# First block of layer 1 in a two-layer attention kernel: bank order, engine orders, three projections kept in their banks, first expert layer in halves

## The chip, the cores and the metric

The kernel runs on one core of one Trainium2 chip. The core has TensorE (PE: matmuls and transposes; its weight loads are listed as PEld), VectorE (DVE), ScalarE (ACT), GpSimd (POOL), and SyncE (SP), which issues the DMAs of this kernel. Each engine takes its instructions in program order and waits on semaphores for those of other engines. TensorE writes to PSUM, which is used here as eight banks of 128 partitions x 512 f32 each.

The metric is the time of one execution in device microseconds. The kernel before took 1599.19 us, the median of three runs (1595.45 to 1604.54).

## The reference, cut to what matters

The input x has 32 x 128 tokens (n, t) of 256 channels, f32. Layer 0 is attention over all 4096 tokens with a mask on t, then an output projection. Layer 1 normalises, adds a windowed attention, normalises again, and adds a mixture of eight experts that all work on every token.

```python
# layer 0, h = x[(1, 32, 128, 256)]
x0 = layernorm(h); q = x0 @ wq.T + bq + sym_emb[n]
Q, K, V = heads(q @ wQ.T + bQ), heads(h @ wK.T + bK), heads(h @ wV.T + bV)   # 8 heads of 32
scores = einsum('bqhd,bkhd->bhqk', Q, K) / sqrt(32)
scores = where(t_key > t_query, -inf, scores)
ctx = einsum('bhqk,bkhd->bqhd', softmax(scores), V)
t = h + alpha * (ctx @ out_w.T + out_b)
...
# layer 1, on t[(1, 4096, 256)]
x = layernorm(t)
logits = relu((x @ K) @ x.T + bias)
window = (i - 12 <= j) & (j < i + 12)
t = t + softmax((logits - 10000 * (1 - window)) * temperature) @ x
x = layernorm(t)
w = softmax(x @ Wr + br)                        # eight weights a token
for e in range(8):
    h1 = relu(bn1(x @ W1[e] + b1[e]))
    h2 = relu(bn2(h1 @ W2[e] + b2[e]))
    t = t + w[:, e] * (h2 @ Wo[e] + bo[e])
```

## The kernel before

**Tiles and blocks.** The 4096 tokens are 32 tiles of 128 (tile n holds the t = 0..127 of one n) and eight blocks of four tiles (`TPB` = 4, 512 tokens). Block b is tiles 4b to 4b+3. `groups[b]` is the same shifted by one, tiles 4b+1 to 4b+4 (tiles 0 to 4 for b = 0), because the window of a tile reaches 16 tokens (`SIDE`) into the next one.

**Layer 0** runs first, over blocks, groups of four heads and key tiles; it fills most of the first 750 us. At its end `close_sums` makes the last softmax sums in one bank; DVE takes their reciprocals in three parts (L1327) and multiplies them into the last columns of `big_t` (L1328), which then holds the attention output, transposed.

**Layer 1, its first block.** It is written out by hand, a list of calls in the order in which every engine gets its instructions (L1915 to 1985). The steps of a tile or a pair of tiles, with their lines:

- `project` (L1533): two matmuls of 256 columns, one for each half of the 256 channels (`project_half`), the output projection of layer 0; DVE adds the residual (L1543), `tile_stats` takes mean and variance (L1528, L1529).
- `deviations` in two parts: part 0 adds eps on DVE (L1515) and takes the square root on ACT (L1518); part 1 is the reciprocal and mean times it, negated, on DVE (L1520, L1521). One call covers several tiles. The Sqrt and the Exp of ACT are in different tables, so a load of 1.28 us stands where they alternate.
- `normalise` (L1560): ACT writes xl, the normalised tile. Then two DMAs on SP copy its first and last 16 rows (L1564, L1566) into the tiles xh of the neighbours, one for two tiles.
- `turn` (L1571, L1572): two transposes on PE, a copy to `big_t` on ACT.
- `key` (L1580, L1585): half of the keys of a block, two matmuls of 512 columns, copy on ACT.
- `logits` (L1592; DVE L1607, 1612, 1613): 160 scores for each token of a tile, threshold and mask, minus the maximum. `exponentials` (L1619) on ACT.
- `turn_weights` (L1628 to 1634): for a pair of tiles, three transposes of the softmax weights, then a copy on ACT (L1633) and one on DVE (L1634) to ptl.
- `apply` (L1641, L1645, L1651): weights times xl, then weights times the side rows xh, for two tiles; DVE divides, adds the residual and takes the next statistics.
- `expert_tokens` (L1683, xf on DVE), `turn_tokens` (L1692, four transposes; L1696, the copy to half of xfT on ACT): the input of the experts for two tiles.
- `route` (L1704, L1709): 8 small matmuls for the router's logits.

**Layer 1, the loop.** For each block and each of eight experts: `layer` W2 of this expert (L1760, four matmuls of 512 columns; relu on ACT, L1765), a call of `insert()`, `layer` W1 of the next expert, `insert()`, `combine` (L1779, L1787), `insert()`. So there are 24 points a block. `insert()` places jobs of the blocks to come, the same steps as above: it goes through the list in order, takes at most four a point, each at least one point after the jobs that it needs, and takes one that has a cost only while the cost spent is below an even share:

```python
    POINTS = 3 * E * (NBLK - 1) - 8
    total = sum(j[1] for j in jobs)
    ...
            if cost and spent >= total * (point + 1) / POINTS:
                k += 1
                continue
```

In the first block, tiles 0 to 15 are projected, and tiles 0 to 6 normalised and turned, before the loop starts; the rest are jobs.

**Banks.** `bank()` gives the PSUM bank of each of these steps from three pools, "h" with three banks, "y" with two and "x" with three, in the order of `spare["tags"]`; in the loop it gives "x" only. A bank that is given again waits until its last readers are done.

**Queues.** SP issues, in this order: K of the layer-1 attention (Ksb), tokens of block 4, Wr (L1488, after POOL has cleared its tile, which POOL does after 16 calls of `with_bias`, L904), br, bo, the expert weights (L1477, 24 loads of 256 KB) with three token loads between them (L896), and then the xh copies as `normalise` calls them. POOL adds the output bias to tokens (`with_bias`) and makes the shifts of the batch norms (L1667 to 1670).

## Time and profile before

| what | value |
|---|---|
| median of three runs | 1599.19 us (1595.45 to 1604.54) |
| the profiled execution | 1596.23 us |
| its span, first to last instruction | 1594.2 us |
| mean granted TensorE clock | 0.990 |
| busy time PE | 1532.1 us, 96% of the span |
| busy time DVE, ACT, POOL | 885.3, 878.7, 106.7 us |
| chain of work that ended last, PE's share | 88% |
| layer 0 until the last sums are closed (first 747 us) and layer 1 after it (847 us) | 1594 us |

The page also cuts the span into slices (40 slices of 39.9 us, busy share in tenths, then the granted clock in tenths, DMA's busy share and GB/s):

```profile
PE   7899899999999999998789999999999999999998
PEld 5333232232222222222446556565565656556555
DVE  4676779888898898998623223233232432223211
ACT  3666777878878878986343433334333333333322
POOL 1110003000000000003400000000000000000000
PEclk9999999999999999999889999999999999999999
DMA  4210000000000010000600000000000000000000
```

PE is at eight or nine tenths nearly everywhere. The slices that matter here are the nineteenth to the twenty-first: there DVE falls from nine tenths to two or three, as layer 0 ends, PE falls to seven or eight, its clock to eight, and the DMA engines have their one busy slice after the start, with the expert weights.

The granted clock is the share of its full rate at which TensorE was allowed to run. A matmul record of 256 columns comes every 0.2165 us at full clock and every 0.4265 us at half; an f32 matmul of this kernel leaves two records, a transpose one.

### The profile page before, as it was taken

Reading aid. Unit: us, or ns where it says so; the run is one execution under the profiler, and the core shown is the slowest. Engines: PE = TensorE matmul, PEld = TensorE weight load, DVE = VectorE, ACT = ScalarE, POOL = GpSimd, SP = SyncE. Lnnn points to the kernel's source line nnn. Section 1 sums busy time; section 2 is a strip of 40 time slices with the busy share of each in tenths; the row PEclk is TensorE's granted clock in tenths of the full one; section 3 lists DMA queues with packets and bytes.
Section 4 is the critical chain, followed back from the end, with each engine's and each line's share of the span. In section 5 each row is a group of like instructions: output and inputs, shape, how many; then the busy total and the mean of one; then the engine's idle time right before and its main releaser. Section 6 shows DMA issues by size and latency. Waiting matters only on the chain.

```text
span 1594.2 us, 20898 instructions
## 1 busy us (share of the span) xinstructions
PE 1532.1 (96%) x8163; PEld 707.6 (44%) x8163; DVE 885.3 (56%) x1508; ACT 878.7 (55%) x1162; POOL 106.7 (7%) x295
## 2 busy tenths in 40 slices
PE   7899899999999999998789999999999999999998
PEld 5333232232222222222446556565565656556555
DVE  4676779888898898998623223233232432223211
ACT  3666777878878878986343433334333333333322
POOL 1110003000000000003400000000000000000000
PEclk9999999999999999999889999999999999999999
DMA  4210000000000010000600000000000000000000
GB/s 107 61 28 18 21 8 24 8 21 8 2 8 8 1 47 21 1 8 21 203 4 4 14 1 4 14 0 17 0 0 17 1 9 8 1 15 0 14 0 15
DMA packets 36343, 30.51 MB, mean 19 GB/s; under 512 B 10007, under 2 KB 34318, under 8 KB 36238
## 3 DMA queue, kind: packets, MB, share of 16 engines
q1 hardware_dynamic: 35088, 28.02, 6.3%
q8 instruction: 66, 1.08, 0.3%
q10 hardware_dynamic: 1150, 1.09, 0.3%
q14 instruction: 39, 0.32, 0.1%
HBM read 23.63 MB, written 4.32 MB: 18 GB/s over the span
## 4 chain that ended last, share of the span: by engine, by line
PE 88%; ACT 4%; DVE 2%; issue 2%; DMA 1%; POOL 1%; SPq 0%; DVEq 0%; POOLq 0%; ACTq 0%
PE psh L1760 28%; PE sa L1246 16%; PE av L1290 14%; PE psy L1779 14%; PE psq L981 2%; ACT pt L1260 2%; PE psv L996 2%; PE psk L968 2%; PE psk L1580 2%; PE sb L1246 1%; ACT pt L1258 1%; PE sums L1316 1%; PE pso L1533 1%; PE pss L1592 1%; DMA tokens<-in_x_dram 1%
## 5 line engine op out<-in xcount | busy, mean ns | idle before, releaser
L1280 DVE TENSOR_TENSOR acc<-acc,pt 128x1024 f32<-128x1024 f32 (+3 forms) x500 | 525.1, 1116 | 43.8 <-ACT pt L1260 31.7
L1765 ACT ACTIVATE h<-psh,bshift,bscale 128x512 f32<-128x512 f32 x256 | 198.6, 776 | 395.1 <-PE psh L1760 395.1
L1260 ACT ACTIVATE pt<-sb 128x1536 f32<-128x1536 f32 (+3 forms) x288 | 387.6, 1346 | 3.3 <-PE sb L1246 3.2
L1246 PE MATMUL sa<-q,kT 32*128 32x512 f32 (+3 forms) x576 | 302.2, 604 | 7.3 <-ACT pt L1258 5.3
L1246 PE MATMUL sb<-q,kT 32*128 32x512 f32 (+3 forms) x1728 | 306.1, 604 | 2.2 <-ACT pt L1260 1.1
L1290 PE MATMUL av<-pt,v 128*32 128x512 f32 (+3 forms) x2304 | 286.2, 569 | 2.7 <-POOL pt L1264 1.3
L1787 DVE SCALAR_TENSOR_TENSOR tokens<-psy,w,tokens 128x256 f32<-128x256 f32 x256 | 111.9, 479 | 260.0 <-PE psy L1779 259.9
L1760 PE MATMUL psh<-xfT,W_sb 128*128 128x512 f32 x512 | 233.7, 599 | 0.7 <-ACT xfT L1696 0.7
L1779 PE MATMUL psy<-Wo_sb,h 128*128 128x256 f32 x1024 | 233.0, 380 | 0.4 <-ACT h L1765 0.4
L1760 PE MATMUL psh<-h,W_sb 128*128 128x512 f32 x512 | 231.4, 595 | 0.0
L1258 ACT ACTIVATE pt<-sa 128x512 f32<-128x512 f32 (+3 forms) x288 | 162.3, 563 | 95.1 <-PE sb L1246 70.9
L1779 PEld LDWEIGHTS psy<-Wo_sb,h 128*128 128x128 f32 x1024 | 192.1, 190 | 40.3 <-issue 16.1
L1246 PEld LDWEIGHTS sa<-q,kT 32*128 32x128 f32 x576 | 84.2, 183 | 217.5 <-ACT pt L1258 178.1
L1760 PEld LDWEIGHTS psh<-xfT,W_sb 128*128 128x128 f32 x512 | 95.6, 192 | 111.7 <-issue 109.0
L1760 PEld LDWEIGHTS psh<-h,W_sb 128*128 128x128 f32 x512 | 94.9, 190 | 99.0 <-issue 96.2
L1290 PEld LDWEIGHTS av<-pt,v 128*32 128x32 f32 x2304 | 45.4, 108 | 201.8 <-issue 182.8
L1264 POOL MEMSET pt<- 32x128 f32 (+2 forms) x192 | 58.5, 304 | 658.9 <-ACT pt L1260 574.5
L1246 PEld LDWEIGHTS sb<-q,kT 32*128 32x128 f32 x1728 | 88.0, 183 | 9.5 <-ACT pt L1260 6.9
L1280 DVE TENSOR_TENSOR acc<-pt,pt 128x1024 f32<-128x1024 f32 (+1 forms) x32 | 36.7, 1188 | 35.5 <-ACT pt L1260 30.6
L1607 DVE SCALAR_TENSOR_TENSOR s<-pss,negb,bandb 128x144 f32<-128x144 f32 x64 | 16.1, 293 | 53.7 <-PE pss L1592 53.7
L1651 DVE SCALAR_TENSOR_TENSOR tokens<-psa,sum,tokens 128x256 f32<-128x256 f32 x32 | 14.9, 466 | 53.0 <-PE psa L1645 53.0
L1533 PE MATMUL pso<-woT,big_t 128*128 128x256 f32 x128 | 38.3, 441 | 5.2 <-DVE rec_last L1327 5.2
(219 smaller groups left out, 911.8 us busy)
## 6 DMA issues: line engine op xcount, KB each, us to landing
xg<-in_x_dram SPq DMA_DIRECT2D x32, 128.0 KB
tokens<-in_x_dram SPq DMA_DIRECT2D x8, 512.0 KB
W_sb<-in_L_ffn_W_dram SPq DMA_DIRECT2D x16, 256.0 KB
out_dram<-tokens SPq DMA_DIRECT2D x32, 128.0 KB
rec<-flat SPq DMA_DIRECT2D x60, 64.0 KB
xs<-in_x_dram SPq DMA_DIRECT2D x24, 128.0 KB
Wo_sb<-in_L_ffn_Wo_dram SPq DMA_DIRECT2D x8, 256.0 KB
xh<-xl SPq DMA_DIRECT2D x62, 16.0 KB
```

The lines of the kernel that those rows point to most:

```text
L968: nc.tensor.matmul(ps, lhsT=wKT[:, c, g * P : (g + 1) * P], rhs=hT[:, c, :], start=(c == 0), stop=(c == 1),)
L1246: nc.tensor.matmul((sb[:, h - 1, :] if h else sa)[:, lo:], lhsT=kT[rows, g, j * P : (j + 1) * P], rhs=q[rows, g, lo:], start=True, stop=True,)
L1258: nc.scalar.activation(pt[:, 0, lo:], sa[:, lo:], AF.Exp, scale=SCALE)
L1260: nc.scalar.activation(pt[:, 1:, lo:], sb[:, :, lo:], AF.Exp, scale=SCALE)
L1264: nc.gpsimd.memset(pt[k * N : (k + 1) * N, :, lo : lo + k * N], 0.0)
L1280: nc.vector.tensor_tensor(live[b, g][:, hs, lo:], old[:, hs, lo:], pt[:, hs, lo:], op=ALU.add)
L1290: nc.tensor.matmul(av[h * HD : (h + 1) * HD, lo:], lhsT=v[:, j, (g * HG + h) * HD : (g * HG + h + 1) * HD], rhs=pt[:, h, lo:], start=(j == ...
L1533: nc.tensor.matmul(ps, lhsT=big_t[:, c, SIDE + n * P : SIDE + (n + 1) * P], rhs=woT[:, c, :], start=(c == 0), stop=(c == 1),)
L1760: nc.tensor.matmul(ps, lhsT=W[name][:, e, c, m * P : (m + 1) * P], rhs=src[:, c, :], start=(c == 0), stop=(c == 1),)
L1765: nc.scalar.activation(dst[:, m, :], ps, AF.Relu, bias=bshift[:, m, k : k + 1], scale=bscale[:, m, k : k + 1],)
L1779: nc.tensor.matmul(ps[:, k, :], lhsT=ht[:, c, r * P : (r + 1) * P], rhs=W["Wo"][:, e, c, :], start=(c == 0), stop=(c == 1),)
L1787: nc.vector.scalar_tensor_tensor(out=tokens(n), in0=ps[:, k, :], scalar=w[:, r, e : e + 1], in1=tokens(n), op0=ALU.mult, op1=ALU.add,)
```

## The change

It does six things:

1. The order of the bank tags becomes x, x, h, x, and then a cycle; the first four banks of the first block then lie outside the pool banks in which the last sums were made. Four tiles, not five, have their two matmuls apart; tile 4 is projected whole, after them.
2. The calls of the first block come in another order: the first two `normalise` ahead of the second `deviations`; three more together; `key` ahead of the projections of tiles 7 and 8 and of the batch norms; `logits(1)` ahead of `exponentials(0)`; the second `turn_weights` ahead of the square root of the second norm; `expert_tokens` earlier.
3. Tiles 9, 10 and 11 are projected into banks where they stay (`kept`); DVE adds and measures them after both halves of xf.
4. The first layer of the first expert is computed in two halves of 256 columns (`layer_halves`), the first of them before the second half of xfT is turned. `route(0)` comes after it as before.
5. The projections of tiles 12 to 15, and normalise and turn of tiles 5 and 6, are jobs of the loop instead.
6. `insert()` asks `allowed()`: the cost of block b's jobs is due by point 24b - 10, evenly between these marks.

```diff
@@ -1464,7 +1464,7 @@
     ps_h = ctx.enter_context(tc.tile_pool(name="ps_h", bufs=3, space=PSUM))
     ps_y = ctx.enter_context(tc.tile_pool(name="ps_y", bufs=2, space=PSUM))
     ps_x = ctx.enter_context(tc.tile_pool(name="ps_x", bufs=3, space=PSUM))
-    spare = {"tags": itertools.cycle("xhyxhyxh")}
+    spare = {"tags": itertools.chain("xxhx", itertools.cycle("yhxyhxhx"))}
 
     def bank(name):
         tag = next(spare["tags"])
@@ -1535,11 +1535,13 @@
             start=(c == 0), stop=(c == 1),
         )
 
-    def project(n, ps=None):
-        if ps is None:
-            ps = bank(f"pso{n}")[:, :D]
-            project_half(n, 0, ps)
-        project_half(n, 1, ps)
+    def project(n):
+        ps = bank(f"pso{n}")[:, :D]
+        for c in range(2):
+            project_half(n, c, ps)
+        finish(n, ps)
+
+    def finish(n, ps):
         nc.vector.tensor_tensor(tokens(n), ps, tokens(n), op=ALU.add)
         tile_stats(n, "st6b_")
 
@@ -1751,6 +1753,28 @@
         for r, ps in both:
             n = b * TPB + r
             nc.vector.tensor_tensor(tokens(n), ps, tokens(n), op=ALU.add)
+
+    def layer_halves(src, name, l, b, e, parts=2):
+
+        pss = [ps_h.tile([P, BLK], F32, tag="h", name=f"psh{l}_{b}_{e}_{m}") for m in range(2)]
+        for part in range(parts):
+            cols = slice(part * BLK // parts, (part + 1) * BLK // parts)
+            for m in range(2):
+                for c in range(2):
+                    nc.tensor.matmul(
+                        pss[m][:, cols], lhsT=W[name][:, e, c, m * P : (m + 1) * P],
+                        rhs=src[:, c, cols], start=(c == 0), stop=(c == 1),
+                    )
+            if part < parts - 1:
+                yield
+        dst = fh.tile([P, 2, BLK], F32, tag=f"h{l}", name=f"h{l}_{b}_{e}")
+        k = l * E + e
+        for m in range(2):
+            nc.scalar.activation(
+                dst[:, m, :], pss[m], AF.Relu,
+                bias=bshift[:, m, k : k + 1], scale=bscale[:, m, k : k + 1],
+            )
+        yield dst
 
     def layer(src, name, l, b, e):
         dst = fh.tile([P, 2, BLK], F32, tag=f"h{l}", name=f"h{l}_{b}_{e}")
@@ -1912,77 +1936,87 @@
     def tiles(b):
         return range(b * TPB, (b + 1) * TPB)
 
-    halves = {n: bank(f"pso{n}")[:, :D] for n in groups[0]}
-    for n in groups[0]:
+    first_free = 0
+
+    def project_next():
+        nonlocal first_free
+        project(first_free)
+        first_free += 1
+
+    def whole(n):
+
+        ps = bank(f"pso{n}")[:, :D]
+        for c in range(2):
+            project_half(n, c, ps)
+        return ps
+
+
+    halves = [bank(f"pso{n}")[:, :D] for n in range(TPB)]
+    for n in range(TPB):
         project_half(n, 0, halves[n])
-    for n in groups[0]:
-        project(n, halves.pop(n))
+    for n in range(TPB):
+        project_half(n, 1, halves[n])
+        finish(n, halves[n])
         if n == 1:
             deviations(range(0, 2), 0)
         if n == 2:
             deviations(range(0, 2), 1)
-    first_free = groups[0][-1] + 1
-
-    def project_next():
-        nonlocal first_free
-        project(first_free)
-        first_free += 1
-
-    deviations(range(2, TPB + 1), 0)
     normalise(0)
     normalise(1)
+    project(TPB)
+    first_free = TPB + 1
+    deviations(range(2, TPB + 1), 0)
     turn(0)
     turn(1)
-    project_next()
     deviations(range(2, TPB + 1), 1)
-    normalise(2)
+    for n in range(2, TPB + 1):
+        normalise(n)
     project_next()
     turn(2)
-    normalise(3)
+    project_next()
     turn(3)
-    normalise(4)
+    turn(4)
     for b in range(TPB, NBLK):
         for n in tiles(b):
             with_bias(n)
-    turn(4)
+    key(0, 0)
+    key(0, 1)
     project_next()
     project_next()
     deviations(groups[1], 0)
     batch_norms()
-    key(0, 0)
-    key(0, 1)
     deviations(groups[1], 1)
-    project_next()
-    project_next()
+
     logits(0)
+    logits(1)
     exponentials(0)
-    logits(1)
     exponentials(1)
-    project_next()
     logits(2)
     exponentials(2)
+    kept = [(first_free, whole(first_free))]
     turn_weights(0)
     logits(3)
     exponentials(3)
-    project_next()
+    kept.append((first_free + 1, whole(first_free + 1)))
     apply(0)
+    turn_weights(1)
     deviations(range(0, 2), 0)
-    turn_weights(1)
-    project_next()
+    kept.append((first_free + 2, whole(first_free + 2)))
+    apply(1)
     deviations(range(0, 2), 1)
+    deviations(range(2, TPB), 0)
     expert_tokens(0, 0)
-    project_next()
-    apply(1)
-    deviations(range(2, TPB), 0)
-    turn_tokens(0, 0)
-    for n in groups[1][:2]:
-        normalise(n)
     deviations(range(2, TPB), 1)
     expert_tokens(0, 1)
-    for n in groups[1][:2]:
-        turn(n)
-    project_next()
+    turn_tokens(0, 0)
+    for n, ps in kept:
+        finish(n, ps)
+    first_free += len(kept)
+    a = layer_halves(blk[0]["xfT"], "W1", 0, 0, 0)
+    next(a)
     turn_tokens(0, 1)
+    a = next(a)
+    route(0)
 
 
 
@@ -1993,7 +2027,7 @@
 
     for n in range(first_free):
         done_at["project", n] = -9
-    for n in range(groups[1][2]):
+    for n in groups[0]:
         done_at["normalise", n] = done_at["turn", n] = -9
     for g in (0, 1):
         done_at["dev0", g] = done_at["dev", g] = -9
@@ -2076,12 +2110,30 @@
 
 
     work = [(b, e) for b in range(NBLK) for e in range(E)]
-    a = layer(blk[0]["xfT"], "W1", 0, 0, 0)
-    route(0)
     spare["tags"] = itertools.cycle("x")
-    POINTS = 3 * E * (NBLK - 1) - 8
-    total = sum(j[1] for j in jobs)
     point, spent = 0, 0.0
+
+
+
+    dues, share = [(0, 0.0)], {b: 0.0 for b in range(1, NBLK)}
+    for name, cost, f, needs in jobs:
+        own = isinstance(name, tuple) and isinstance(name[1], int)
+        b = name[1] if own else 1
+        if own and name[0] in ("project", "normalise", "turn"):
+            b = max(1, (b - 1) // TPB)
+        elif own and name[0] in ("logits", "exp"):
+            b //= TPB
+        elif own and name[0] in ("weights", "apply"):
+            b //= TPB // 2
+        share[b] += cost
+    for b in range(1, NBLK):
+        dues.append((3 * E * b - 10, dues[-1][1] + share[b]))
+
+    def allowed():
+        for (p0, c0), (p1, c1) in zip(dues, dues[1:]):
+            if point < p1:
+                return c0 + (c1 - c0) * (point + 1 - p0) / (p1 - p0)
+        return dues[-1][1]
 
     def insert():
 
@@ -2089,7 +2141,7 @@
         k = few = 0
         while k < len(jobs) and few < 4:
             name, cost, f, needs = jobs[k]
-            if cost and spent >= total * (point + 1) / POINTS:
+            if cost and spent >= allowed():
                 k += 1
                 continue
             if all(done_at.get(q, point) < point for q in needs if q in known):
```

## The prediction

> **What bounds the kernel now.** I read the windows by engine first, to see which stretch can be shortened at all; the columns are the stretch, its length, busy time and count of PE, PE weight load, DVE, ACT and POOL, then granted clock, DMA share and GB/s.
>
> ```profile
> core 0: us, PE busy (x) PEld busy (x) DVE busy (x) ACT busy (x) POOL busy (x), PEclk, DMA share, GB/s
> 747.60:764.50 16.90, 7.62 (x24) 5.83 (x20) 11.24 (x25) 0.27 (x2) 13.30 (x22) 0.80 0.23 73
> 764.50:787.60 23.10, 18.36 (x69) 13.19 (x69) 12.00 (x42) 8.88 (x21) 13.56 (x22) 0.85 0.96 309
> 787.60:812.20 24.60, 17.06 (x68) 9.65 (x67) 11.54 (x42) 7.16 (x17) 0.00 (x0) 0.72 0.02 4
> 812.20:1594.20 782.00, 774.53 (x2774) 463.65 (x2767) 228.17 (x715) 285.30 (x450) 6.63 (x36) 1.00 0.02 7
> ...
> ```
>
> From 812.2 to the end PE is busy 774.53 of 782.00 us at full clock: the loop over experts costs what its matmuls cost, and work moved into it pays its whole PE time. Only the 64.6 us before it have slack, PE being busy 43.0 of them, part of that at a clock of 0.72 to 0.85.
>
> Second, PE's timeline in that stretch (start, duration, line, tiles, count; in brackets the idle time and who ended it):
>
> ```profile
> 752.84 7.55 PE L1533 MATMUL pso<-woT,big_t 128*128 128x256 f32 x20 [5.18 <-DVE rec_last L1327]
> 765.23 1.18 PE L1571 MATMUL ptx<-ident,xl 128*128 128x128 f32 x4 [4.84 <-ACT xl L1560]
> ...
> 776.49 3.60 PE L1580 MATMUL psk<-big_t,Ksb 128*128 128x512 f32 x8
> ...
> 788.16 1.13 PE L1641 MATMUL psa<-xl,ptl 128*128 128x256 f32 x4 [0.36 <-ACT ptl L1633]
> 789.22 0.70 PE L1645 MATMUL psa<-xh,ptl 32*128 32x256 f32 x4
> ...
> 794.60 1.13 PE L1641 MATMUL psa<-xl,ptl 128*128 128x256 f32 x4 [2.34 <-ACT ptl L1633]
> ...
> 801.63 1.18 PE L1571 MATMUL ptx<-ident,xl 128*128 128x128 f32 x4 [4.02 <-ACT xl L1560]
> ...
> 806.05 5.71 PE L1760 MATMUL psh<-xfT,W_sb 128*128 128x512 f32 x8 [0.68 <-ACT xfT L1696]
> ...
> 812.26 0.70 PE L1760 MATMUL psh<-h,W_sb 128*128 128x512 f32 x1
> ```
>
> The waits of 5.18, 4.84, 2.34 and 4.02 us are what the change aims at. The start at 812.26 is the mark I follow: what the head gains is how much earlier this second expert layer (W2) starts.
>
> Third, the queue that issues the side rows xh, which apply's L1645 reads:
>
> ```profile
> 780.16 0.37 SPq L1477 DMA_DIRECT2D Wo_sb<-in_L_ffn_Wo_dram  x1
> 780.97 0.54 SPq L1566 DMA_DIRECT2D xh<-xl  x1
> 781.72 0.53 SPq L1564 DMA_DIRECT2D xh<-xl  x1
> 782.43 0.51 SPq L1566 DMA_DIRECT2D xh<-xl  x1
> 783.22 0.51 SPq L1564 DMA_DIRECT2D xh<-xl  x1
> ```
>
> The xl of these rows were written from 764.58 on, but the copies are issued only at 780.97, behind the last expert weights. Their records in the trace show landings at 787.13, 787.30, 787.46 and 787.63 for the first four (the fourth is the last that apply(0) reads) and 788.29 for the eighth, the last that apply(1) reads. In the slices of 779 to 789 us the DMA engines are at 9 tenths until about 785, so the small copies wait behind weights. Before the change L1645 ran at 789.22, only 1.59 us after its landing; nobody had to wait.
>
> **The change part by part.**
>
> *Banks outside the last sums' set.* The instruction order with its waits shows the first projection of the changed kernel still behind the DVE's last reciprocal (L1327), with the same wait values as before. So 752.84 stays. What remains is that four first halves instead of five precede the first second half: one matmul, two records. The x14 of 752.84 to 758.92 take 6.08 us at a clock of 0.50, 0.43 each: first DVE add at 758.41 - 0.85 = 757.56.
>
> *Engine orders, early part.* Before, ACT took the square root of tiles 2 to 4 (764.43, after a 3.27 us wait) ahead of xl of tiles 0 and 1 (764.58), though their nmr was ready at 762.17. Now xl 0 and 1 come first: tiles 0 to 2 take 3 x 1.02 us of DVE (0.42 + 0.43 + 0.18) from 757.56, the deviations some 0.7, so xl at about 761.4, 3.2 us earlier. xl 2 to 4 follow in one go at about 764.6, not 769.6 to 773.0. Key then has only two projections ahead of it instead of four and starts at about 767.2, not 776.49: 9.3 us early. SP's and POOL's queue orders up to here are as before (one memset of POOL comes later). With logits at 771 to 776, and no projections between them on DVE, apply(0)'s L1641 ends between 780 and 783.
>
> *What is late next.* PE takes its work in order, and L1645 waits for the fourth side row. Weight loads and xh stand in the same order on SP, whose start (757.71) hangs on POOL's L904 and whose pace hangs on saturated DMA, neither of which the change touches. So L1645 starts at 787.63 against 789.22: of 9.3 us gained, 1.6 remain. Queued behind it on PE are the transposes of the second pair's weights, two kept projections, apply(1) and all that follows; POOL waits for none of it. PE idles 5 to 7 us there, so the clock will fall: the trace grants 0.50 in 796.47 to 810.12, after waits of 4 us and less.
>
> *From 787.63 to the loop,* at full clock, and at half in brackets (256-column records 0.2165 [0.4265] us, transposes 0.109 [0.213]). L1645 and the second pair's transposes, then its copies without the 1.28 us table load and 0.20 us square root that stood ahead of them at 792.79: apply(1) at 790.5, not 794.60. Its first tile is done after six of eight records, 791.9 [793.1]; DVE needs 2 x 1.05 for both tiles, 0.2 for eps, so xf at 794.3 [795.5]; xf 2 x 0.37; four transposes and the 0.58 copy plus 0.1: first half of xfT at 796.3 [797.75]. Eight records of the half layer 1.73 [3.41], four transposes 0.44 [0.85], copy 0.7: second half at 799.2 [802.8]. Eight records, 0.1 and a relu of 0.78: W2 at 801.8 [807.1]. Kept projections cost PE nothing on this path (they fit in the wait for xh, 4 x 0.22 to 0.43 us each), and their DVE work, 3 x 1.02 us, is behind xf and under the half layers, 3.5 us at least; without that cover up to 3.1 us. Route in the prefix moves 16 records, 0.65 us, under the relu. A whole layer behind the second copy (eight records of 0.43 [0.85] us) would end one part later, so the halves are worth 1.7 [3.4] us of this.
>
> Which clock? Of the path from 788 to 802 the matmuls are about 7 us at full speed, and the rows nearest to it, 787.6 to 812.2, were granted 0.72 with less waiting ahead. I take W2 at 805.5, near the half-clock end: 812.26 - 805.5 = 6.7 us gained, with bounds 5.2 and 10.5.
>
> The rule that speaks against the change is in the Trainium skill, "TensorE: Matmul & The Clock Gate", section "What's actually happening": the throttled state is the default, and one idle window of about 3.4 us brings half rate. The rows agree in kind (0.50 over 796.47 to 810.12); by the page alone every matmul after the xh wait runs at half, W2 starts at 807.1, and the sum below is -1.3.
>
> *Moved into the loop.* Projections 12 to 15: 4 x 4 records x 0.2165 = 3.46 us. Turns of tiles 5 and 6: 2 x 2 x 0.109 = 0.44 us. Their add, stats, xl and copies go to DVE and ACT, busy 228 and 285 of 782 us there; their four xh DMAs to an SP queue that is nearly empty (DMA share 0.02). Sum 3.9 us, all paid.
>
> *Due per block.* Block 1's jobs are now due by point 14, a rate above the even pace of 160 points. Banks x are three, a point takes at most four jobs. Lower bound 0 (7.47 us is all the idle PE has in the loop, and part of it might go, so at best a gain of 1); upper bound: a wait like that of 2.34 us before L1641 at a few of the first 24 points. I take 0, with 3 as the bound, since DVE and ACT are idle over 60% of the loop.
>
> **Sum:** -6.7 + 3.9 + 0 = -2.8 us; with the bounds -10.5 + 3.9 - 1 = -7.6 and -5.2 + 3.9 + 3 = +1.7. The profiled execution took 1596.23 us (span 1594.2, 2 us around it); the median of the runs is 1599.19 (1595.45 to 1604.54). I set the difference against the median: 1599.19 - 2.8 = 1596.4. The scatter of the runs is larger than this difference. About 0.5%, 8 us, is what a measurement of this kernel can tell from no change.
>
> **The rivals.**
>
> *xh doesn't bind* (0.15). If the copies land by 782, because SP reaches them earlier or DMA is less crowded, everything after 787.63 shifts by up to 5 us and the clock has less idle time to fall: W2 at 796 to 802, the sum -12.3 to -6.3, 1587 to 1593. For it: the copies are 16 KB each. Against: issue at 780.97 behind 24 weight loads that no edit moves, and the DMA engines busy to 785.
>
> *The denser first block stalls the loop* (0.07), the other side. By the costs that the code gives its jobs, 27 us of them fall due in the first 24 points, where 17 did; key, logits and weights chains then wait for ACT and DVE at their place in PE's order. One such wait is 2.34 us (weights before L1641) to 4.02 us (transposes before xl); to be over 0.5% slower the waits must add 8 + 2.8 = 11 us, five at 2.34. Then 1608 to 1612. For it: those very waits exist in the prefix, where the same chain has nothing to hide under. Against: at each point of the loop a whole expert layer, 8 records of 0.43 us, stands between a job and the one that needs it.
>
> *The change doesn't do what it says* (0.2). The bank edit is such a case already. If in addition the clock stays at 0.50 and the half layers wait for each other, W2 starts at 807 to 809 and the gain of 3 to 5 us equals the 3.9 us moved: 1598 to 1600.
>
> **How the numbers follow.** My forecast has 0.58, the rivals 0.15, 0.07 and 0.2. Likeliest 1596.4, its own range 1592 to 1601. The range for 8 in 10 adds the first rival's middle and half the scatter of a median: 1589 to 1602. Faster by over 0.5% (below 1591.2) needs the larger half of the first rival or a lucky median: 0.10. Slower by over 0.5% (above 1607.2): the second rival, 0.06. The same: 0.84.
>
> **What would show it.** In the changed profile: PE's first projection still ended by rec_last; xl at about 761.4 and key at about 767; L1645's successor preceded by 5 to 7 us of idle PE ended by a DMA of xh near 787.6; xh issues still from 780.97; clock near 0.50 from then until the loop; W2 between 801.8 and 807; PE's busy time in the loop 3.9 us more and its idle time still near 7.5. I would be wrong if xh lands before 783, if the clock holds at 1.00 after the wait, or if idle PE in the first 24 points of the loop grows by over 3 us.

## The result, and the profile after

The changed kernel takes 1597.59 us (median of 14 runs, 1593.13 to 1602.61), the kernel before 1597.22 us (14 runs, 1594.06 to 1604.54). The ratio is 1.0001 with a 95% interval of 0.9986 to 1.0016, which is -2.2 to +2.6 us: no change that can be measured. The profiled execution has a span of 1594.5 us at a clock of 0.990, against 1594.2 us and 0.990.

The start of the last sums of layer 0 is a better mark than the start of the span. In the fourteen profiles of this study it (the row `sums<-acc`) lies between 746.37 and 751.23 us, and two kernels that are the same up to there differ by 4.8 us. So I split each profile at two points: **head** is from that row to the start of W2, the second expert layer; **loop** is from there to the end of the span. Before, the head took 812.26 - 746.62 = 65.64 us and the loop 1594.2 - 812.26 = 781.94 us, 847.58 together. The changed kernel's PE timeline gives its two marks (start, duration, tiles, count; in brackets the idle time and who ended it):

```profile
748.08 1.04 PE L1316 MATMUL sums<-acc,ones 128*32 128x512 f32 x8
754.28 7.40 PE L1533 MATMUL pso<-woT,big_t 128*128 128x256 f32 x20 [5.16 <-DVE rec_last L1327]
764.46 0.93 PE L1573 MATMUL ptx<-ident,xl 128*128 128x128 f32 x4 [2.78 <-DVE st6b L1528]
...
769.16 3.70 PE L1582 MATMUL psk<-big_t,Ksb 128*128 128x512 f32 x8 [0.24 <-ACT big_t L1574]
...
784.02 1.03 PE L1643 MATMUL psa<-xl,ptl 128*128 128x256 f32 x4
788.40 1.45 PE L1647 MATMUL psa<-xh,ptl 32*128 32x256 f32 x4 [3.35 <-DMA xh<-xl]
...
797.82 1.11 PE L1694 MATMUL ptf<-ident,xf 128*128 128x128 f32 x4 [2.94 <-DVE xf L1685]
799.61 3.78 PE L1764 MATMUL psh<-xfT,W_sb 128*128 128x256 f32 x8 [0.68 <-ACT xfT L1698]
803.18 1.06 PE L1694 MATMUL ptf<-ident,xf 128*128 128x128 f32 x4
804.91 1.99 PE L1764 MATMUL psh<-xfT,W_sb 128*128 128x256 f32 x8 [0.68 <-ACT xfT L1698]
806.84 0.65 PE L1706 MATMUL psr<-xfT,Wr 128*32 128x128 f32 x16
807.41 3.70 PE L1784 MATMUL psh<-h,W_sb 128*128 128x512 f32 x8
```

The first projection still waits for the last reciprocal. The wait of 4.84 us for xl has become 2.78, and the key comes at 769.16, 14.9 us after the first projection and not 23.7. Then a wait of 3.35 us for a DMA of xh stands in the middle, where there was none. W2 starts at 807.41: the head is 807.41 - 748.08 = 59.33 us, 6.31 less than before.

The windows by engine of the same profile (stretch, its length, then busy time of PE, its weight load, DVE, ACT, POOL; granted clock, DMA share, GB/s):

```profile
785.05:788.40 3.35, 0.00 (x0) 0.03 (x1) 0.00 (x0) 0.00 (x0) 1.68 (x2) 0.84 0.49 149
788.40:794.20 5.80, 5.80 (x17) 3.59 (x17) 2.43 (x10) 1.86 (x3) 0.00 (x0) 0.50 0.04 10
...
807.41:1594.50 787.09, 778.76 (x2791) 467.26 (x2787) 232.72 (x727) 278.49 (x448) 6.85 (x37) 1.00 0.02 7
```

The loop takes 787.09 us, 5.15 more than before; PE is busy 778.76 of it, 4.29 more, and idle 8.33, 0.86 more. So the head gave 6.31 and the loop took 5.15: 1.16 us less in these two stretches, which the interval of the ratio holds. What was gained at the head was nearly all paid back.

### The profile page after: what moved, and what is told of

The parts are those of the page before. It is cut to its first block, busy times and chain, and to the rows that moved or that the text cites. A ratio compares the mean times of both kernels' runs of the same rounds, so it can differ in the third digit from the quotient of the medians.

```text
span 1594.5 us, 20904 instructions
## 1 busy us (share of the span) xinstructions
PE 1533.4 (96%) x8171; PEld 711.1 (45%) x8171; DVE 886.9 (56%) x1508; ACT 870.0 (55%) x1156; POOL 106.7 (7%) x295
## 4 chain that ended last, share of the span: by engine, by line
PE 89%; ACT 4%; DVE 3%; issue 2%; DMA 1%; POOL 0%; ACTq 0%; DVEq 0%; SPq 0%; POOLq 0%
PE psh L1784 28%; PE sa L1246 16%; PE av L1290 14%; PE psy L1803 14%; PE psq L981 2%; ACT pt L1260 2%; PE psk L1582 2%; PE psv L996 2%; PE pso L1533 2%; PE psk L968 2%; PE sb L1246 1%; PE sums L1316 1%; ACT pt L1258 1%; PE pss L1594 1%; PE psa L1643 1%
## 5 line engine op out<-in xcount | busy, mean ns | idle before, releaser
L1784 PE MATMUL psh<-xfT,W_sb 128*128 128x512 f32 x504 | 227.2, 593 | 0.0
```

What stands on the lines that cost most here:

```text
L1784: nc.tensor.matmul(ps, lhsT=W[name][:, e, c, m * P : (m + 1) * P], rhs=src[:, c, :], start=(c == 0), stop=(c == 1),)
```

## The experiments

Each was timed in five rounds beside the kernel before. The table collects head and loop from each profile, one profile a kernel; the sections say what they tell. Steps ahead of an edit differ between profiles too, by up to 1.3 us, so a difference in head of about a microsecond is the edit's only if it also shows when the time is counted from a mark just ahead of the edit.

| kernel | head | loop | sum | ratio to before (95%) |
|---|---|---|---|---|
| before | 65.64 | 781.94 | 847.58 | 1 |
| the change | 59.33 | 787.09 | 846.42 | 1.0001 (0.9986 to 1.0016) |
| e8, before with the dues | 65.88 | 781.80 | 847.68 | 1.0005 (0.9992 to 1.0018) |
| e2, before, xh first | 65.28 | 782.45 | 847.73 | 0.9998 (0.9985 to 1.0011) |
| e1, change, xh first | 54.98 | 787.19 | 842.17 | 0.9963 (0.9950 to 0.9976) |
| e9, change, xh on ACT's queue | 65.03 | 787.01 | 852.04 | 1.0049 (1.0034 to 1.0064) |
| e3, change, projections put back | 57.29 | 782.61 | 839.90 | 0.9957 (0.9939 to 0.9974) |
| e5, change, other pools | 57.81 | 786.73 | 844.54 | 0.9993 (0.9982 to 1.0004) |
| e4, change, whole layer | 58.47 | 787.04 | 845.51 | 0.9990 (0.9980 to 1.0001) |
| e12, change, turn first | 56.44 | 787.16 | 843.60 | 0.9988 (0.9979 to 0.9997) |
| e6, e1 and projections back | 53.44 | 783.82 | 837.26 | 0.9930 (0.9913 to 0.9948) |
| e7, e6 and e5 | 50.36 | 783.85 | 834.21 | 0.9917 (0.9900 to 0.9934) |
| e10, e7, logits ahead on DVE | 47.61 | 784.06 | 831.67 | 0.9907 (0.9889 to 0.9925) |
| e11, e10, turn first, two adds later | 46.09 | 783.48 | 829.57 | 0.9896 (0.9881 to 0.9910) |

### What xh waits for: e1, e2, e9

e1 and e2 move the bulk of the loads behind the xh copies of tiles 0 to 4, in the changed kernel and in the one before:

```diff
-    for b in range(5, NBLK):
-        load_tokens(b, res.tile([P, TPB, D], F32, name=f"tokens{b}"))
-        load_expert(b - 3)
-    for e in range(NBLK - 3, E):
-        load_expert(e)
+    def load_rest():
...
     for n in range(2, TPB + 1):
         normalise(n)
+    load_rest()
     project_next()
```

> The changed kernel, with the loads of experts 2 to 7 and of token blocks 5 to 7 issued on SP after the xh copies of tiles 0 to 4. Queue theory (xh stands behind the weights on SP, and that took the gain of the new order): xh lands over 10 us earlier, the second matmuls of apply(0) follow the first without the 3.35 us wait, W2 starts 47 to 50 us after the first projection (53.13 in the changed kernel), 3 to 6 us less in all, ratio to before 0.996 to 0.998. Rival (the chain through DVE and ACT sets W2, the wait only takes its place): W2 within 1 us of 53.1, ratio 0.9995 to 1.0005.

> The kernel before with the same move of the loads. Queue theory: there apply(0) came 1.59 us after its xh had landed, so nothing is gained: W2 59.4 us after the first projection, within 1 us, ratio 0.9990 to 1.0010. Rival (crowded DMA or SP slows the first block in some other way): W2 over 2 us earlier here too.

The loads are the same; only their place on SP differs. SP's first xh copy in the change, then the first two in e1, then PE's timeline in e1:

```profile
782.46 0.54 SPq L1568 DMA_DIRECT2D xh<-xl  x1
```

```profile
763.78 0.54 SPq L1569 DMA_DIRECT2D xh<-xl  x1
764.41 0.53 SPq L1567 DMA_DIRECT2D xh<-xl  x1
```

```profile
784.12 1.31 PE L1644 MATMUL psa<-xl,ptl 128*128 128x256 f32 x4
785.36 0.70 PE L1648 MATMUL psa<-xh,ptl 32*128 32x256 f32 x4
...
795.13 3.56 PE L1765 MATMUL psh<-xfT,W_sb 128*128 128x256 f32 x8 [0.67 <-ACT xfT L1699]
```

The second matmuls follow the first at once. The head is 54.98 us, 4.35 less than the change, and the loop is the same to 0.1: 0.9963. In the kernel before the same move does nothing (65.28 against 65.64, 0.9998), though xh is issued some 16 us earlier there too, and in both the second matmuls follow the first without a wait. That zero is a sum: in e2 apply(0) starts 43.51 us after the sums, 1.97 later than before, with the key taking 4.71 us instead of 3.60, and the whole expert layer, 3.70 us instead of 5.71, gives it back; why is not shown. So the wait is made by the change: the new order of the engines is worth 6.3 us of head as it is, and 65.28 - 54.98 = 10.3 us when xh is out of its way. The rival, that the DVE and ACT chain would take the wait's place, falls.

e9 leaves the loads and issues those nine copies from ACT:

```diff
+        queue = nc.scalar if n <= TPB else nc.sync
         if n:
-            nc.sync.dma_start(out=beside(n - 1)[:SIDE], in_=xls[n][:SIDE])
+            queue.dma_start(out=beside(n - 1)[:SIDE], in_=xls[n][:SIDE])
```

> The changed kernel with the xh copies of tiles 0 to 4 issued by ACT on its own queue; the loads stay first on SP and the DMA engines stay crowded. Queue theory (the order on SP's queue is what delays xh): xh lands before 780 and apply(0) doesn't wait, W2 as in e1 (54 to 57 us after the last sums began on acc), ratio 0.996 to 0.9985; ACT gives some of it back, about 0.5 us a copy. Crowding theory (the DMA engines full of weights delay them on any queue): apply(0) waits for xh until after 786, W2 at 59 or later, ratio 0.999 to 1.002.

Half of it came true. The copies are issued from 766.87 to 777.92, while the weights still stream. The fourth, the last that apply(0) reads, landed at 777.29 (788.59 in the change), and apply(0) doesn't wait for it. But ACT's timeline shows what it costs:

```profile
766.87 0.61 ACTq L1569 DMA_DIRECT2D xh<-xl  x1
767.52 0.60 ACT L1562 ACTIVATE xl<-tokens,nmr,rstd 128x256 f32<-128x256 f32 x1 [4.51 <-DMA W_sb<-in_L_ffn_W_dram]
...
771.36 0.21 ACT L1518 ACTIVATE rstd<-rstd 128x3 f32<-128x3 f32 x1 [3.23 <-DMA W_sb<-in_L_ffn_W_dram]
```

The first copy follows its xl by 3.9 us, and ACT stands still 4.51 and 3.23 us for landings of weights. In the trace the DMAs of both queues take turns on eight completion semaphores, and a DMA waits for the one eight before it: the loads eight places ahead of four of the copies landed at 766.77, 769.32, 770.77 and 773.06, and these copies were issued at 766.87, 769.39, 770.79 and 773.14. So on ACT's queue a small copy still waits for a load, and now xl, copies and exponentials wait behind it. The head is 65.03 us and the kernel 0.49% slower. The order on the queue was the cause of the late xh, but another queue is no remedy.

### What the loop paid: e8, e3

e8 takes the new pacing alone into the kernel before:

```diff
-            if cost and spent >= total * (point + 1) / POINTS:
+            if cost and spent >= allowed():
```

> The kernel before with the dues per block alone. Theory (the 5.15 us that the loop grew are the moved matmuls, 4.29 us of PE, and under 1 us of waits): the loop within 1 us of 781.9, the head unchanged, ratio 0.999 to 1.001. Rival (the denser first block costs by itself): the loop 2 us or more longer, ratio over 1.001.

The loop took 781.80 us, 0.14 less:

```profile
815.20:1597.00 781.80, 774.27 (x2771) 463.74 (x2767) 228.65 (x715) 276.59 (x444) 6.84 (x37) 1.00 0.02 7
```

In the kernel before, the dues are free; no run takes them out of the changed kernel.

e3 does the projections before the loop again, where PE waits for xh:

```diff
-    kept = [(first_free, whole(first_free))]
+    project_next()
     turn_weights(0)
     logits(3)
     exponentials(3)
-    kept.append((first_free + 1, whole(first_free + 1)))
+    for _ in range(5):
+        project_next()
     apply(0)
     turn_weights(1)
     deviations(range(0, 2), 0)
-    kept.append((first_free + 2, whole(first_free + 2)))
+    kept = [(first_free, whole(first_free))]
     apply(1)
```

> The changed kernel with projections 9 to 14 done whole before apply(0), where PE waits for xh, and 15 kept: nothing of projections moves into the loop. Theory of moved work: PE is busy 3.5 us less in the loop (778.8 to about 775.3), the wait for xh is filled, W2 stays within 1.5 us of 53.1 after the first projection, 3 to 5 us less in all, ratio 0.997 to 0.998. Rival (their add and statistics on DVE delay apply and the chain after it): W2 2 to 4 us later than 53.1 and ratio 0.9995 to 1.0005.

```profile
805.59:1588.20 782.61, 775.06 (x2775) 464.06 (x2771) 228.61 (x715) 281.45 (x450) 6.89 (x37) 1.00 0.02 7
```

PE is busy 775.06 us in the loop, as expected, and the ratio is better than expected, 0.9957. The loop falls to 782.61, 4.48 us less than the change for four projections: 1.12 us each, not the 0.87 of their matmuls. e6, which leaves one of the four in the loop, gives the same: 787.19 (e1) - 783.82 = 3.37 for three, 1.12 each. Profiles with the same jobs in the loop differ by up to 0.58 us (783.48 to 784.06 in e6, e7, e10 and e11), so the price is known to some 0.2 us. And the head is shorter too. PE's timeline and windows of e3:

```profile
782.81 5.61 PE L1533 MATMUL pso<-woT,big_t 128*128 128x256 f32 x20
788.25 1.03 PE L1643 MATMUL psa<-xl,ptl 128*128 128x256 f32 x4
789.21 0.70 PE L1647 MATMUL psa<-xh,ptl 32*128 32x256 f32 x4
```

```profile
788.25:796.13 7.88, 4.64 (x25) 2.96 (x23) 6.72 (x27) 2.06 (x4) 0.00 (x0) 0.95 0.03 9
```

Five projections fill the place of the wait, and in the stretch behind it the granted clock is 0.95 (1.00 up to 793.26, while PE works), where the change had 0.50 over 788.40 to 794.20. From the second matmuls of apply(0) to W2 it takes 805.59 - 789.21 = 16.38 us instead of 807.41 - 788.40 = 19.01. So the idle wait cost twice: its own 3.35 us, and about 2.6 us of half clock behind it. With projections moved into the loop that could have filled it, the change lost a third time.

### The banks: e5

```diff
-            ps_a = at.enter_context(tc.tile_pool(name="ps_a", bufs=1, space=PSUM))
             ps_b = at.enter_context(tc.tile_pool(name="ps_b", bufs=2, space=PSUM))
+            ps_a = at.enter_context(tc.tile_pool(name="ps_a", bufs=1, space=PSUM))
...
-    ps_y = ctx.enter_context(tc.tile_pool(name="ps_y", bufs=2, space=PSUM))
     ps_x = ctx.enter_context(tc.tile_pool(name="ps_x", bufs=3, space=PSUM))
+    ps_y = ctx.enter_context(tc.tile_pool(name="ps_y", bufs=2, space=PSUM))
-    spare = {"tags": itertools.chain("xxhx", itertools.cycle("yhxyhxhx"))}
+    spare = {"tags": itertools.chain("yyxh", itertools.cycle("xhxyhxhy"))}
```

Tiles 0 and 1 are projected first, both halves, then 2 and 3.

> The changed kernel with the PSUM pools in another order, so that the pool of the first two projections has no bank in common with the pool of the last sums; tiles 0 and 1 are projected first, 2 and 3 after. Theory (the wait hangs on the pool that a bank belongs to, not on the bank): the first projection follows the last sums at once, about 5 us earlier, and xl of tile 0 comes 3 to 4 us earlier; the xh copies still land at the same time, so W2 starts within 1.5 us of 59.3 us after the last sums began (L1316, 59.33 in the changed kernel) and the ratio is 0.999 to 1.001. Rival (the late start is what counts): W2 about 4 us earlier, ratio 0.997 to 0.998.

PE's timeline of e5:

```profile
746.66 1.04 PE L1316 MATMUL sums<-acc,ones 128*32 128x512 f32 x8
747.64 1.13 PE L1533 MATMUL pso<-woT,big_t 128*128 128x256 f32 x4
749.32 1.13 PE L1533 MATMUL pso<-woT,big_t 128*128 128x256 f32 x4 [0.56 <-DVE big_t L1328]
...
786.27 1.49 PE L1647 MATMUL psa<-xh,ptl 32*128 32x256 f32 x4 [5.27 <-DMA xh<-xl]
```

The first projections follow the sums with no wait, the second halves wait 0.56 us for their own columns. So the bank of the tile was not what counted: bank 5, which the change gave to tile 0, lies outside banks 1 to 3 of the sums, but its pool in layer 0 (`ps_b`, six banks) is the one the sums were in, and the wait is for the last reader of that pool. Measured from the sums the first projection comes 5.2 us earlier (0.98 instead of 6.20) and the first transposes of xl 4.5 us (11.85 instead of 16.38), and the wait for xh grows from 3.35 to 5.27 us: only 1.5 us of head are left at W2, and the ratio is 0.9993 (0.9982 to 1.0004). The theory held, at its edge for W2, and the first xl came a little earlier than the 3 to 4 us it gave.

### The halves: e4, e12

```diff
-    a = layer_halves(blk[0]["xfT"], "W1", 0, 0, 0)
-    next(a)
     turn_tokens(0, 1)
-    a = next(a)
+    a = layer(blk[0]["xfT"], "W1", 0, 0, 0)
```

> The changed kernel with the first expert layer whole again, after the second half of xfT. Theory (halves hide one half layer under the turn and copy of the second tokens): W2 1.7 to 3.5 us later than 59.33 after the last sums (acc), the loop as in the changed kernel, 787.1, ratio to before 1.001 to 1.0025. Rival (the halves only fill time in which the whole layer would have waited for the clock anyway): W2 within 0.7 us, ratio 0.9995 to 1.0010.

Neither held: with the layer whole again the head is 58.47 us, 0.86 shorter than with halves. The timeline of the change shown first tells why: the second transposes (803.18) are called after the first half layer and stand behind it on PE, so PE waits out one copy before each half, 0.68 us twice, and hides nothing. e12 calls the turn first:

```diff
     a = layer_halves(blk[0]["xfT"], "W1", 0, 0, 0)
-    next(a)
     turn_tokens(0, 1)
+    next(a)
     a = next(a)
```

> The changed kernel with the second turn of tokens called ahead of the first half layer instead of after it. Theory (the halves as written hide nothing: the second turn stands behind the first half on PE, so each half waits out one copy of 0.58 us): W2 1.0 to 1.8 us earlier than 59.33 after the last sums (acc) and about 0.7 earlier than the whole layer's 58.47; loop 787.1; ratio to before 0.998 to 1.000. Rival (the halves are slow only because of the granted clock): W2 within 0.5 us of 59.33.

```profile
800.69 2.03 PE L1694 MATMUL ptf<-ident,xf 128*128 128x128 f32 x8 [2.94 <-DVE xf L1685]
802.52 4.31 PE L1764 MATMUL psh<-xfT,W_sb 128*128 128x256 f32 x16
```

Eight transposes and sixteen records in one run, no wait between them. The head is 56.44 us: 2.03 less than the whole layer, 2.89 less than the change. The three are alike up to the key, which starts 21.08 us after the sums in the change and 21.09 in e4 and e12. It is more than I expected: the two waits of 0.68 us are 1.36 of it, and the run without gaps also gets the full clock back sooner: 0.68 over 802.5 to 804.5 us and 1.00 after it, where the change has 0.53 over 797.80 to 804.80. The halves were right; their place in the order was not. The ratio is 0.9988 (0.9979 to 0.9997), 1.9 us; the timed runs do not tell e12 from e4 (0.9990), only the profiles do.

### Together: e6, e7, e10, e11

e6 is e1 with projections 12 to 14 put back into PE's gap after apply(1), and 9 and 10 added by DVE before apply(0). e7 adds the pools of e5.

> The changed kernel with both: loads behind xh as in e1, and projections 12 to 14 put back before the loop, whole, in PE's idle 2.94 us between apply(1) and the first transposes of xf; 9 and 10 are added and measured by DVE before apply(0). Only 15 stays a job. Theory (two separate losses, the wait for xh in the head and 0.87 us a projection in the loop): W2 within 1.5 us of the 54.98 us after the last sums (acc) that e1 had, the loop 2.6 us shorter than e1's 787.2, PE's clock higher behind the filled gap, ratio to before 0.994 to 0.9955. Rival (one loss, seen twice: once xh is early there is no room for the projections, and they delay the chain by what they save): W2 2.5 us later than in e1, ratio as e1, 0.9963.

> e6 with the pools of e5, so that the first two projections no longer wait for the last reciprocal. With xh early nothing hides an earlier start: theory, W2 2.5 to 4 us earlier than in e6, ratio 0.9915 to 0.994. Rival (DVE, which still does all three reciprocals before the first add, sets the pace): W2 within 1 us of e6, ratio as e6.

The core of e6's edit (e7's is the sum of those above):

```diff
+    nine = whole(9)
     turn_weights(0)
     logits(3)
     exponentials(3)
+    ten = whole(10)
+    finish(9, nine)
+    finish(10, ten)
     apply(0)
...
     apply(1)
     deviations(range(0, 2), 1)
+    kept += [(n, whole(n)) for n in range(12, 15)]
```

The two losses are separate, as the theory said, and e6 gave more than expected: a head of 53.44 us, 1.5 less than e1 though PE does more in it, and a loop 3.37 less; 0.9930. Of the 1.5 us, 1.28 are already there at the second matmuls of apply(0) (36.75 us after the sums, 38.03 in e1), up to which PE's order is the same in both; behind them the head is 0.26 shorter. So e6's edit leaves the head as it is, and what it gains is the loop. In e7, with xh early, the earlier start is worth 3.08 us of head, where e5 had 1.5; 0.9917.

e10 takes DVE's work on projections 7 and 8, the deviations of the second group and the batch norms from between the key and the logits:

```diff
-    project_next()
-    project_next()
-    deviations(groups[1], 0)
-    batch_norms()
-    deviations(groups[1], 1)
+    early = [(n, whole(n)) for n in (7, 8)]
     logits(0)
     logits(1)
```

> e7 with DVE's work on projections 7 and 8, the deviations of the second group and the batch norms put behind the logits of the first block (7 to 10 are added before apply(0), the deviations and norms after xf). Theory (in e7 the logits, ready on PE, wait 2 to 2.5 us for DVE, and this is on the path): W2 1.5 to 2.5 us earlier than e7's 50.36 after the last sums, the loop within 0.5 us of 783.85, ratio to before 0.9900 to 0.9915. Rival (the DVE work only moves to a place where it delays apply(0) as much): W2 within 0.7 us of 50.36, ratio 0.9910 to 0.9925.

The head is 47.61 us, 2.75 less than e7, a little over the range. But only part of it is the edit's. The windows from the first transposes of xl to the key, ahead of all that e10 changes, in e7, e10 and e11:

```profile
761.12:768.22 7.10, 5.04 (x19) 3.52 (x19) 4.41 (x12) 3.29 (x9) 2.45 (x4) 0.74 0.61 187
763.07:768.86 5.79, 3.52 (x18) 2.44 (x18) 4.20 (x12) 3.34 (x10) 2.44 (x4) 0.99 0.54 157
758.35:765.30 6.95, 4.84 (x19) 3.29 (x19) 4.42 (x12) 3.30 (x10) 2.45 (x4) 0.79 0.64 182
```

The clock granted there was 0.99 in e10 and 0.74 in e7, and e10's key starts 1.30 us earlier (17.63 us after the sums, 18.93 in e7). From the key to W2 e10 gains 1.45 us (29.98 instead of 31.43), just under the range. e11 is e10 with the turn of e12, and with 9 and 10 added after the second pair's weights:

```diff
-    finish(9, nine)
-    finish(10, ten)
     apply(0)
     turn_weights(1)
     deviations(range(0, 2), 0)
...
+    finish(9, nine)
+    finish(10, ten)
     apply(1)
```

> e10 with the second turn ahead of the first half layer, and projections 9 and 10 added by DVE after the second pair's weights instead of before apply(0). Theory (in e10 the copy of the second pair's weights stands behind four projections on DVE, and the second copy of xfT is exposed): apply(1)'s second matmuls 1.5 to 2.5 us earlier, W2 2.5 to 4 us earlier than e10's 47.61 after the last sums, the loop within 0.5 us of 784.1, ratio to before 0.988 to 0.990. Rival (the added work only changes place): W2 within 1 us of 47.61, ratio 0.990 to 0.9915.

Counted from the sums it is a miss in size: 1.52 us of head, not 2.5 to 4, and apply(1)'s second matmuls come 0.61 us earlier instead of 1.5 to 2.5 (35.09 us after the sums, 35.70 in e10). But e11's clock ahead of the key was 0.79, and its key starts 1.14 us later than e10's. Counted from the key, both are in the range: the second matmuls 1.75 us earlier (16.32 instead of 18.07), W2 2.66 (27.32 instead of 29.98). DVE's timeline of e11 shows what is left:

```profile
782.57 0.39 DVE L1546 TENSOR_TENSOR tokens<-pso,tokens 128x256 f32<-128x256 f32 x1
782.99 0.43 DVE L1529 BATCH_NORM_STATS2 st6b<-tokens 128x6 f32<-128x256 f32 x1
783.46 0.18 DVE L1530 BATCH_NORM_AGGREGATE mean<-st6b 128x2 f32<-128x6 f32 x1
783.55 0.45 DVE L1654 SCALAR_TENSOR_TENSOR tokens<-psa,sum,tokens 128x256 f32<-128x256 f32 x1
```

No row has idle time in front: DVE works without a break from 775.94 to the end of xf at 787.6, and what is moved within that stretch only changes place. There it is now DVE that sets the head. e11 still beats both kernels: 1580.18 us (4 runs, 1578.22 to 1581.36), 0.9896 with 0.9881 to 0.9910.

## Why the prediction was right, and where it was not

The measured time, 1597.59 us, lies in the range of 1589 to 1602, and it is the case that had a chance of 0.84, no change that can be told. The forecast was 2.8 us less than before; the profiles give 1.16 less, the ratio nothing that can be told from zero. That the forecast of 1596.4 lies 1.2 us from the result is partly luck: it started from a median of three runs, 1599.19, where fourteen give 1597.22, and this makes up for most of a gain that was put too high. By its steps:

- **The bound.** Right: the loop is PE's work, and what is moved there is paid. e8 and e3 show that of the 5.15 us the loop grew, the dues took none (in the kernel before) and the four projections 4.48. The size was off: 3.9 predicted. A projection in the loop costs about 1.12 us, not the 0.87 of four records. In PE's busy time e3 saves 3.70 of 4.48 (778.76 against 775.06); the rest is idle time. Of the 1.25 us by which the loop was mis-sized, 0.39 is busy time and 0.86 idle time, for which the prediction chose 0. In the first 86.6 us of the loop PE is idle 0.69 us, where it was never idle before. That is far below the 3 us that would have shown the prediction wrong. By the code's costs some 22 us of jobs fall due by point 24, where 15 did, not the 27 and 17 of the prediction.
- **The banks.** Right, and taken in: the wait stayed at 5.16 us. e5 shows the reason, which the prediction didn't have.
- **The early orders.** Key 14.9 us after the first projection, predicted 767.2 - 752.84 = 14.4. The first xl came 9.5 us after it, 8.6 predicted; the eps step of 1.24 us in the last section is the difference. But "with logits at 771 to 776, and no projections between them on DVE" was wrong: projections 7 and 8, the deviations and the batch norms hold DVE from 773.83 to 777.68 in the changed kernel, and from the key to W2 e10 gained 1.45 us by moving them. So L1643 ended at 785.05, 30.8 us after the first projection, where 27 to 30 was said, and the wait was 3.35 us instead of 5 to 7.
- **xh is late next.** Right, in place and time: issued from 782.46, behind the weights, the second matmuls 34.1 us after the first projection (787.63 - 752.84 = 34.8 predicted). e1 and e2 show that this wait took 4.35 us of the gain. Of the three kept projections only the third stands behind the wait (790.48), not two; it still cost nothing there, since apply(1) started (792.18) when DVE's copy of its weights had ended (792.13).
- **The clock.** Right: 0.50 from 788.40 to 794.20; W2 came 53.1 us after the first projection, 52.7 predicted, with bounds of 49.0 and 54.3. The bound of 54.3, everything after the wait at half, is not what the page alone says, as the prediction has it. In the Trainium skill, "TensorE: Matmul & The Clock Gate", section "What's actually happening", about 3.4 us of sustained work brings back the full rate. The rows agree with that half of the rule too: after the 5.80 busy us the clock is 0.97, and at the end, where the second half layer and route run, 1.00.
- **The halves.** Wrong. "The halves are worth 1.7 [3.4] us" of the gain; in fact, called as they are, they cost 0.86 (e4). The chain was worked out correctly, with a transposes-and-copy step between the parts; the whole layer beside it was not: there both turns run before the layer, and that step is not between anything.
- **The sum.** Head 6.3 (6.7 predicted), loop 5.15 (3.9): the difference of 1.6 us is mostly the loop's price for a projection.

Of the rivals, "xh doesn't bind" was false for the change and was then made true in e1: 1591.95 us (1591.55 to 1593.08), inside the 1587 to 1593 it was given. The denser block did not stall the loop (e8, and the 0.69 us above). That the change doesn't do what it says was true of the banks and of the halves. And 0.5% was too coarse for what can be told: the intervals here reach 0.1 to 0.2% to either side.

## What to carry to other kernels

When a chain is moved earlier, ask first which transfer it will meet, and look at that transfer's place on its queue: nine copies of 16 KB behind 24 weight loads of 256 KB ate 4.35 us here, and with 18 of those loads behind them the same reordering, which had shown nothing, made the kernel 0.37% faster (0.24 to 0.50%). An idle wait on PE is a place for work that is off the path: filled with projections it saved their price in the loop and the half clock behind it. And a layer cut in halves hides nothing until the work that feeds the second half stands ahead of the first.

## What I had not expected of the hardware

The granted clock answers late. In the change's windows it is still 0.84 in the 3.35 us in which PE does nothing, 0.50 in the next 5.80, in which PE is busy throughout, 0.97 in the 3.60 after that, in which PE is busy 0.68, and falls again when the transposes start. The full clock that the busy stretch had earned was granted to an idle engine. e12 shows it again, 0.95 over the 2.94 us in which PE waits for xf and 0.50 over the first 1.81 us of its work. The change:

```profile
794.20:797.80 3.60, 0.68 (x5) 0.28 (x4) 2.71 (x11) 0.20 (x1) 0.00 (x0) 0.97 0.00 0
797.80:804.80 7.00, 5.75 (x16) 4.05 (x16) 3.94 (x14) 1.11 (x2) 0.00 (x0) 0.53 0.00 0
804.80:807.40 2.60, 2.49 (x24) 1.81 (x24) 0.00 (x0) 1.29 (x3) 0.00 (x0) 1.00 0.00 0
```

Tiny DVE instructions can take seven times as long. In the change, the eps step of two numbers a partition took 1.24 us at 761.13 and 0.17 us (three numbers) at 765.67. POOL was adding biases from 759.58 to 762.34, and not at 765.67:

```profile
759.58 2.76 POOL L904 TENSOR_TENSOR tokens<-tokens,outb 128x256 f32<-128x256 f32 x4
...
761.13 1.24 DVE L1515 TENSOR_SCALAR rstd<-mean 128x2 f32<-128x2 f32 x1
...
765.67 0.17 DVE L1515 TENSOR_SCALAR rstd<-mean 128x3 f32<-128x3 f32 x1
```

This instruction is on the path to the first xl, and it ended when POOL's batch did, within 0.05 us; three more long ones (0.55 to 0.61 us instead of 0.16, L1521 and L1615) also fall under POOL's adds, while reciprocals and statistics there keep their length. The fourteen profiles together show how closely the two go together. These three kinds of instruction (eps, mean times reciprocal, and in L1615 the row maximum times minus the temperature) ran 876 times with no two-operand POOL instruction beside them and took 0.14 to 0.17 us each time. They ran 104 times beside one and took up to 1.87 us, and each of the 66 that took over 0.25 us ended within 0.03 us of the end of a POOL instruction. The Trainium skill, "SBUF — State Buffer", section "SBUF: two separate sides", says that VectorE and GpSimd share one pair of ports which the first to come holds for its whole instruction; no run here took POOL's work away, so the cause is not shown.

That layer 0, the same in most of these kernels, ends up to 4.8 us earlier or later from one profile to the next is left unexplained; it is four times the 1.16 us that this change made.
